# Tanh rows of additive attention: the column groups of one fill go to VectorE or GpSimd one by one

## The chip, the cores and the metric

The kernel runs on one core of a Trainium2 chip. The metric is the device time of one execution in microseconds (us). A core has four compute engines with instruction queues of their own: TensorE (PE in the profile, its weight loads PEld), VectorE (DVE), ScalarE (ACT) and GpSimd (POOL). Each works through its queue in order; between engines, semaphores hold an instruction until the data that it reads is there and the buffer that it writes is free. SyncE (SP) issues most DMAs.

## The reference

Everything is float32. There are 8 batches of 1024 tokens with 128 channels. Layer 0 is a convolution-like attention with 8 heads and two softmaxes, a layer norm, a feed-forward block and another layer norm. Layer 1 is what the change touches: additive attention, and then a recurrence.

```python
def _L1_attn_ref(B, W, v):
    Wi = jnp.einsum('bnd,ed->bne', B, W)
    scores = jnp.einsum('d,bijd->bij', v, jnp.tanh(Wi[:, None, :, :] + Wi[:, :, None, :]))
    attn = jax.nn.softmax(scores, axis=-1)
    return jnp.einsum('bij,bjd->bid', attn, B)

def step(yt, wx_t):                      # the recurrence, over 1024 tokens
    yt = jax.nn.sigmoid(wx_t + yt @ Vt)
    return (yt, yt)
```

For each pair (i, j) of tokens of a batch there are 128 sums, 128 tanh values and a weighted sum over the channels with `v`. The scores are symmetric in i and j, so the kernel computes one triangle.

## The kernel before

Channels lie on the 128 partitions, so `wiT` holds `Wi` of a batch as 128 x 1024. Token i gives one row: `tanh(wiT[:, i0:] + wiT[:, i])`. The 1024 tokens are cut into 8 row tiles `it` of 128 tokens. Row tile `it` needs w = 1024 − 128·it columns (a little less as one goes down in it, since the triangle starts at `begin[c]`). A **group** (function `group`, from line 978) is four **columns groups** c = 0 to 3 with k rows each, where k is 1 for row tiles 0 to 3, 2 for 4 and 5, 4 for 6, and 8 for 7. All of a group lies in one slot of the ring `th`, which has five slots of 128 x 4096 (three of them serve the first batch's narrow tiles).

A group can be made in two ways.

- ACT makes it directly (`tanh_row`, L1001): one tanh instruction for each row, with `wiT[:, i]` as its bias.
- DVE or POOL fills the slot with the sums, and then ACT does one wide tanh over the whole slot in place (L1047). POOL fills with one `tensor_tensor` for each of the four columns (`add_rows`, L1011). DVE fills with one `tensor_scalar` with an accumulator for each row where k is below 4 (`add_row`, L1005; the profile shows it as TENSOR_SCALAR_CACHE_REDUCE with a DVE_READ_ACCUMULATOR behind it), and with `add_rows`, four instructions, where k is 4 or 8.

Then PE multiplies the group's rows with `v` (`times_v`, L1064): the matmuls collect 128 tokens' scores in the PSUM tile `sa`, and the last one sets the slot free. When a pair of row tiles is complete, ACT takes the exponential out of `sa` (L1160), and the attention to B and the layer norm follow.

The order on every engine is not written by hand. The class `Plan` collects operations (`add`) with the engines that may do each, an estimated cost on each of them, a priority `pri`, what it reads and writes, and the slot that it takes or gives back. `emit` then plays the schedule through in Python when the program is built: it takes the engine that could start soonest, and among the operations that could start on it within 0.15 us of that the one with the lowest priority number, a handicap added that an engine's entry may carry. Only the resulting order goes to the chip; the chip's own durations decide when things really run. For an operation with several possible engines the choice is made in this play. `behind` holds an operation until others have begun. `port=True` marks DVE operations[...], and the play does not let the two run at once.

Layer 0 of batch b + 1 runs beside layer 1 of batch b; the priorities of both rise by one per batch, so that they advance together. The engines that may make a group are in the list `fillers`, which `layer1` writes for each group:

```python
if wide:
    fillers = [("ACT", 0.0)] + ([] if late else [("POOL", 0.0)]) + ([("DVE", 0.1)] if b < NB - 1 else [])
    if b == NB - 1:
        fillers += [("DVE", 0.1)]
elif it == NT // 2:
    fillers = [("DVE", 0.1), ("ACT", 0.1)] + ([] if late else [("POOL", 0.0)])
else:
    fillers = [("DVE", 0.1)] + ([("ACT", 0.1)] if early else [("POOL", 0.0)])
```

`wide` is row tile 0 to 3, `late` a row tile's last three groups, `early` the first and the last batch. In these two the narrow tiles (5, 6, 7) may thus be begun by DVE or ACT alone. In the other batches narrow row tiles share a pair with wide ones.

Before the change, the first operation of a group chooses among `fillers`, and all others of the group are bound to the engine that did the first (`placed`): 4k rows for ACT, 4k rows or 4 columns for DVE, 4 columns for POOL. Numbers that go beyond that vanish (`where` gives None).

Of the kernel before, what the change touches and what calls it, by code (L numbers as in the profile page):

```python
# [10 lines left out]
AF = mybir.ActivationFunctionType  # L11
# [402 lines left out]
class Plan:  # L414
# [24 lines left out]
    def add(self, where, fn, r=(), w=(), pri=0, mode="full", take=None, give=None, behind=(), wait=(), port=False):  # L439
        n = len(self.ops)  # L440
        deps = set()
        for k in r:
            if k in self.writer:
                deps.add(self.writer[k])
        for k in (*w, *wait):
            if k in self.writer:
                deps.add(self.writer[k])
            deps.update(self.readers.get(k, ()))
        for k in w:
            self.writer[k] = n  # L450
            self.readers[k] = []
        for k in r:
            if k not in w:
                self.readers.setdefault(k, []).append(n)
        deps.discard(n)
        self.ops.append((where, fn, (pri, n), mode, deps, take, give, behind, port))
        self.by.append(None)
        return n
# [107 lines left out]
def fast_path(ctx: ExitStack, tc: tile.TileContext, a: dict, fits):  # L566
# [5 lines left out]
    nc = tc.nc  # L572
# [16 lines left out]
    work = main.enter_context(tc.tile_pool(name="work", bufs=1))  # L589
# [126 lines left out]
    plan = Plan()  # L716
    add = plan.add
# [37 lines left out]
    count = {"aT": 0}  # L755
# [222 lines left out]
    def group(it, at0, r0, k, wiT, all_wi, L1, ROWS, fillers, chain, left, both, first_half):  # L978

        i0 = it * P
        w = N - i0
        g = count.setdefault("group", 0)
        count["group"] = g + 1
        slot = Bank(*slots[: 3 if first_half else 5])

        begin = [0 if r0 == 0 else 4 * r0 + c for c in range(4)]  # L990
        at = [k * sum(w - q for q in begin[:c]) for c in range(5)]

        def rows(c):
            return slot()[:, at[c] : at[c + 1]].rearrange("p (r n) -> p r n", r=k)

        def w_i(c, r=None):
            j = i0 + 4 * r0 + c
            return wiT[:, j : j + 4 * k - 3 : 4] if r is None else wiT[:, j + 4 * r : j + 4 * r + 1]

        def tanh_row(c, r):  # L1000
            nc.scalar.activation(rows(c)[:, r, :], wiT[:, i0 + begin[c] :], AF.Tanh, bias=w_i(c, r))  # L1001

        def add_row(c, r):

            nc.vector.tensor_scalar(  # L1005
                rows(c)[:, r, :], wiT[:, i0 + begin[c] :], w_i(c, r), 0.0, ALU.add, ALU.add, accum_out=unused
            )

        def add_rows(eng, c):
            shape = [P, k, w - begin[c]]  # L1010
            eng.tensor_tensor(  # L1011
                rows(c), wiT[:, i0 + begin[c] :].unsqueeze(1).to_broadcast(shape),
                w_i(c).unsqueeze(2).to_broadcast(shape), ALU.add,
            )


        each = [(c, r) for r in range(k) for c in range(4)]
        work = {
            "ACT": [(0.18 + 0.833e-3 * (w - begin[c]), lambda c=c, r=r: tanh_row(c, r)) for c, r in each],
            "POOL": [  # L1020
                (0.27 + 1.62e-3 * k * (w - begin[c]), lambda c=c: add_rows(nc.gpsimd, c)) for c in range(4)
            ],
            "DVE": [(0.21 + 1.05e-3 * (w - begin[c]), lambda c=c, r=r: add_row(c, r)) for c, r in each]
            if k < 4
            else [(0.15 + 1.04e-3 * k * (w - begin[c]), lambda c=c: add_rows(nc.vector, c)) for c in range(4)],
        }

        def does(i):
            return lambda e: work[e][i][1]()

        first = count[chain] = add(
            [(e, work[e][0][0], x) for e, x in fillers], does(0), r=all_wi, w=[("rows", g, 0)], pri=ROWS,
            take=slot, behind=[count[q] for q in (chain, *both) if q in count], port=k >= 4,
        )

        def placed(i):
            def where():
                e = plan.by[first]
                return (e, work[e][i][0]) if i < len(work[e]) else None

            return where

        for i in range(1, 4 * k):
            add(placed(i), does(i), w=[("rows", g, i)], pri=ROWS, behind=[first], port=k >= 4)
        add(
            lambda: None if plan.by[first] == "ACT" else ("ACT", 0.2 + 0.833e-3 * at[4]),
            lambda _: nc.scalar.activation(slot()[:, : at[4]], slot()[:, : at[4]], AF.Tanh),  # L1047
            r=[("rows", g, i) for i in range(4 * k)], w=[("tanh", g)], pri=ROWS - 0.02,
        )


        parts = []
        for s0 in range(0, N, 512):
            for c in range(4):
                s, s1 = max(s0, at0 + begin[c]), min(s0 + 512, at0 + w)
                if s < s1:
                    parts.append((c, s0, s, s1))
                    left[c, s0] = left.get((c, s0), 0) + k

        def times_v(_):  # L1060
            for r in range(k):
                for c, s0, s, s1 in parts:
                    left[c, s0] -= 1
                    nc.tensor.matmul(  # L1064
                        sa[32 * c : 32 * c + 32, s:s1], vpat[:, 31 - r0 - r : 63 - r0 - r],
                        rows(c)[:, r, s - at0 - begin[c] : s1 - at0 - begin[c]],
                        start=at0 + r0 + r == 0, stop=left[c, s0] == 0,
                    )

        n = -(-w // 512)
        before = ["sa"] if at0 and r0 == 0 else ["sa", "sa narrow"] if at0 else ["sa"] if r0 else []
        after = ["sa narrow"] if at0 and r0 == 0 else [] if r0 or at0 else ["sa"]
        add(
            ("PE", k * (1.69e-3 * (w - begin[0]) + 0.005 * n)), times_v, r=[("tanh", g)] + before,
            w=[("sa", it, r0)] + after, pri=L1, mode="groups", give=slot,
        )
        return ("sa", it, r0)
# [11 lines left out]
    E_first, at = {}, 0  # L1091
# [5 lines left out]
    def layer1(b):  # L1097
# [27 lines left out]
        for pair in order:  # L1125
# [19 lines left out]
            for s, it, at0, r0, k, fillers in sorted(todo):  # L1145
                ROWS = b + (past + n_blocks * s / 33) / len(E_first) / 4.5
                L1 = ROWS - 0.15
                keys.append(group(it, at0, r0, k, wiT, all_wi[:1] if early and pair[0] >= NT // 2 else all_wi, L1, ROWS, fillers, fills[it < NT // 2], left, fills if r0 == 0 else (), b == 0 and pair[0] >= NT // 2))
# [318 lines left out]
```

## Time and profile before

| What | us |
|---|---|
| median of 3 runs | 5683.9 (5677.94 to 5687.07) |
| profiled execution, its own time | 5681.58 |
| its span, first to last instruction | 5679.7 |
| layer 0 of the first batch alone | up to about 310 |
| layer 1 of one batch beside layer 0 of the next | about 392 to 4970 |
| last batch's layer 1, narrow row tiles | about 4970 to 5260 |
| last batch's layer 1, wide row tiles | about 5260 to 5590 |
| recurrence and output | from about 5590 |

The mean granted TensorE clock is 0.968 of full speed. DMA plays no part between the first load and the last stores: the queues took 1.5% or less of the DMA engines' time each.

A line of the groups part reads: source line, engine, operation, out<-in, shape, count | busy us in all, mean ns of one | idle us of the engine just before them, and what ended most of it. "POOL th L1011 <- PE sa L1064" in the waits means that a fill by POOL waited until PE's matmuls had freed its slot.

### The profile page before, as it was taken

How to read it: one execution, taken by the hardware profiler on the slowest of the kernel's cores; microseconds unless marked ns; L12 is line 12 of the kernel's file. 1: busy time of each engine (PE TensorE's matmuls, PEld its weight loads, DVE VectorE, ACT ScalarE, POOL GpSimd, SP SyncE). 2: the span in 40 equal slices, each digit the busy share in tenths (PEclk: the TensorE clock that was granted, in tenths of full speed). 3: DMA queues.
4: the chain of work that ended last, by engine and by line, in shares of the span. 5: the costliest groups of instructions: out<-in, count | busy, mean ns of one | idle time of the engine just before them, and what ended most of it. 6: DMA issues, size and time to landing. Idle time of an engine off the chain costs nothing.

```text
span 5679.7 us, 98799 instructions
## 1 busy us (share of the span) xinstructions
PE 5122.7 (90%) x39013; PEld 2778.3 (49%) x39013; DVE 5230.2 (92%) x8664; ACT 5172.3 (91%) x4498; POOL 4093.4 (72%) x2678
## 2 busy tenths in 40 slices
PE   8999999899999999899999999998998999975567
PEld 6655554545544455445544455554554455532125
DVE  7989999999999999999999999999998999998886
ACT  5489999799998999999999999998898999989994
POOL 2352787678868888778877888788686888862872
PEclk9999999999999999999999999999999999987998
DMA  2000000000000000000000000000000000000001
GB/s 60 1 5 1 1 1 5 1 8 1 1 5 5 5 1 5 1 9 1 1 5 5 5 1 5 1 8 1 1 1 5 5 1 1 11 19 7 1 1 64
DMA packets 27339, 37.88 MB, mean 7 GB/s; under 512 B 2465, under 2 KB 19233, under 8 KB 26865
## 3 DMA queue, kind: packets, MB, share of 16 engines
q1 hardware_dynamic: 24832, 27.99, 1.5%
q8 instruction: 308, 5.05, 0.4%
q10 hardware_dynamic: 1872, 3.16, 0.2%
q14 instruction: 167, 1.36, 0.1%
q0 software_dynamic: 160, 0.33, 0.0%
HBM read 19.41 MB, written 12.06 MB: 6 GB/s over the span
## 4 chain that ended last, share of the span: by engine, by line
PE 48%; DVE 30%; ACT 16%; issue 5%; POOL 1%; DMA 0%; DVEq 0%; ACTq 0%; SPq 0%; POOLq 0%
PE sa L1064 18%; PE m L906 10%; PE sc L857 8%; ACT th L1047 8%; DVE th L1005 7%; PE m L771 5%; ACT th L1001 5%; DVE stat_e L881 4%; DVE wx L868 3%; DVE stat_e L864 3%; DVE aT L783 3%; ACT wx L878 2%; PE m L835 1%; DVE stat_e L882 1%; ACT sc L860 1%
## 5 line engine op out<-in xcount | busy, mean ns | idle before, releaser
L1011 POOL TENSOR_TENSOR th<-wiT 128x1024 f32<-128x1024 f32 (+58 forms) x2088 | 3056.6, 1499 | 676.9 <-PE sa L1064 645.5
L1047 ACT ACTIVATE th<-th 128x3072 f32<-128x3072 f32 (+50 forms) x903 | 2496.1, 2795 | 86.4 <-DVE th L1005 79.0
L1064 PE MATMUL sa<-th,vpat 128*32 128x512 f32 (+34 forms) x24576 | 2079.0, 468 | 254.0 <-ACT th L1047 232.5
L1001 ACT ACTIVATE th<-wiT 128x398 f32<-128x398 f32 (+60 forms) x2444 | 1692.1, 764 | 84.3 <-PE sa L1064 83.2
L1005 DVE TENSOR_SCALAR_CACHE_REDUCE th<-wiT 128x288 f32<-128x288 f32 (+50 forms) x1760 | 1550.4, 881 | 159.4 <-PE sa L1064 44.5
L892 POOL TENSOR_TENSOR wx<-wx,stat_e 128x1024 f32<-128x1024 f32 x512 | 982.3, 1941 | 701.2 <-DVE stat_e L882 526.0
L1064 PEld LDWEIGHTS sa<-th,vpat 128*32 128x32 f32 x24576 | 665.9, 112 | 1427.9 <-issue 868.3
L857 PE MATMUL sc<-xT,wx 128*128 128x512 f32 x2048 | 990.5, 608 | 22.0 <-DVE wx L868 21.4
L906 PE MATMUL m<-aT,wx 128*128 128x256 f32 x3584 | 845.1, 389 | 10.1 <-DVE aT L783 8.7
L906 PEld LDWEIGHTS m<-aT,wx 128*128 128x128 f32 x3584 | 676.8, 193 | 196.5 <-issue 42.8
L868 DVE TENSOR_TENSOR wx<-sc,stat_e 128x1024 f32<-128x1024 f32 x512 | 623.5, 1218 | 23.9 <-DVE stat_e L865 0.5
L864 DVE TENSOR_REDUCE stat_e<-sc 128x16 f32<-128x1024 f32 x512 | 619.7, 1210 | 16.7 <-ACT sc L860 16.2
L783 DVE COPY aT<-m 128x512 f32<-128x512 f32 x932 | 603.1, 672 | 32.9 <-PE m L771 31.0
L771 PE MATMUL m<-ident,wx 128*128 128x128 f32 x3940 | 575.5, 280 | 56.7 <-DVE aT L783 30.2
L771 PEld LDWEIGHTS m<-ident,wx 128*128 128x128 f32 x3940 | 448.4, 142 | 362.9 <-issue 169.7
L860 ACT ACTIVATE sc<-sc 128x1024 f32<-128x1024 f32 x512 | 513.1, 1006 | 98.6 <-PE sc L857 88.2
L881 DVE TENSOR_REDUCE stat_e<-wx 128x128 f32<-128x2048 f32 x256 | 582.8, 2277 | 14.7 <-ACT wx L878 14.3
L878 ACT ACTIVATE wx<-wx 128x2048 f32<-128x2048 f32 x256 | 486.9, 1902 | 71.9 <-DVE wx L868 71.4
L857 PEld LDWEIGHTS sc<-xT,wx 128*128 128x128 f32 x2048 | 354.7, 191 | 403.3 <-issue 337.6
L882 DVE RECIPROCAL stat_e<-stat_e 128x128 f32<-128x128 f32 x256 | 243.9, 953 | 8.8
L739 POOL TENSOR_TENSOR stat<-stat,neg_half 128x4 f32<-128x4 f32 x64 | 65.2, 1019 | 134.8 <-DVE stat L736 115.1
L835 PEld LDWEIGHTS m<-Wvo,xT 128*128 128x128 f32 x1080 | 133.9, 193 | 58.0 <-issue 22.2
(172 smaller groups left out, 3065.7 us busy)
## 6 DMA issues: line engine op xcount, KB each, us to landing
xT<-in_xt_dram SPq DMA_DIRECT2D x8, 512.0 KB, 3.5
th<-in_x_dram SPq DMA_DIRECT2D x8, 512.0 KB, 7.0
parked<-X SPq DMA_DIRECT2D x16, 256.0 KB, 2.3
xr<-parked SPq DMA_DIRECT2D x8, 512.0 KB, 6.8
parked_wx<-bT SPq DMA_DIRECT2D x14, 256.0 KB, 2.0
wx<-parked_wx SPq DMA_DIRECT2D x7, 512.0 KB, 3.3
out_dram<-ot ACTq DMA_DIRECT2D x8, 256.0 KB, 2.2
out_dram<-ot SPq DMA_DIRECT2D x8, 256.0 KB, 2.5
```

Source lines behind the costliest of these rows:

```text
L771: nc.tensor.transpose(bank[:, i * P : (i + 1) * P], s, ident)
L857: nc.tensor.matmul(sc[:, cols], u[:, qt * P : (qt + 1) * P], xT[:, cols], start=True, stop=True)
L864: nc.vector.tensor_reduce(r1, sc.rearrange("p (m g) -> p g m", g=G), AX.X, ALU.add)
L868: nc.vector.tensor_tensor(e3, sc3, r1.unsqueeze(1).to_broadcast([P, M, G]), ALU.mult)
L881: nc.vector.tensor_reduce(r2, e2.rearrange("p q (m g) -> p q m g", g=G), AX.X, ALU.add)
L892: nc.gpsimd.tensor_tensor(e3, e3, r2[:, q, :].unsqueeze(2).to_broadcast([P, M, G]), ALU.mult)
L906: nc.tensor.matmul(bank()[:, :256], vp[:, t, :], aT[:, t, :], start=t == 0, stop=t == NT - 1)
L1001: nc.scalar.activation(rows(c)[:, r, :], wiT[:, i0 + begin[c] :], AF.Tanh, bias=w_i(c, r))
L1005: nc.vector.tensor_scalar(rows(c)[:, r, :], wiT[:, i0 + begin[c] :], w_i(c, r), 0.0, ALU.add, ALU.add, accum_out=unused)
L1011: eng.tensor_tensor(rows(c), wiT[:, i0 + begin[c] :].unsqueeze(1).to_broadcast(shape), w_i(c).unsqueeze(2).to_broadcast(shape), ALU.add,)
L1047: lambda _: nc.scalar.activation(slot()[:, : at[4]], slot()[:, : at[4]], AF.Tanh),
L1064: nc.tensor.matmul(sa[32 * c : 32 * c + 32, s:s1], vpat[:, 31 - r0 - r : 63 - r0 - r], rows(c)[:, r, s - at0 - begin[c] : s1 - at0 - begin ...
```

## The change

A group has four operations now instead of 4k, one for each column c, with all of its k rows. The first still chooses among `fillers`. If ACT takes it, ACT does the other three as well. If not, each of the columns 1 to 3 may go to POOL or to DVE, whatever `fillers` allows the first operation, and without a handicap for either; the play gives it to the one that could start sooner or has nothing more urgent. The wide tanh now reads from `filled` which stretches of the slot were filled. As a group is either ACT's or has all of its columns filled, that is the whole slot or nothing.

```diff
-        each = [(c, r) for r in range(k) for c in range(4)]
+        rows_of = range(k)
         work = {
-            "ACT": [(0.18 + 0.833e-3 * (w - begin[c]), lambda c=c, r=r: tanh_row(c, r)) for c, r in each],
...
+            "ACT": lambda c: (k * (0.18 + 0.833e-3 * (w - begin[c])), lambda: [tanh_row(c, r) for r in rows_of]),
+            "POOL": lambda c: (0.27 + 1.62e-3 * k * (w - begin[c]), lambda: add_rows(nc.gpsimd, c)),
+            "DVE": lambda c: (k * (0.21 + 1.05e-3 * (w - begin[c])), lambda: [add_row(c, r) for r in rows_of])
             if k < 4
-            else [(0.15 + 1.04e-3 * k * (w - begin[c]), lambda c=c: add_rows(nc.vector, c)) for c in range(4)],
+            else (0.15 + 1.04e-3 * k * (w - begin[c]), lambda: add_rows(nc.vector, c)),
         }
-        first = count[chain] = add(
-            [(e, work[e][0][0], x) for e, x in fillers], does(0), r=all_wi, w=[("rows", g, 0)], pri=ROWS,
-            take=slot, behind=[count[q] for q in (chain, *both) if q in count], port=k >= 4,
-        )
...
+        def filled():
+
+            runs = []
+            for c in range(4):
+                if plan.by[ops[c]] != "ACT":
+                    if runs and runs[-1][1] == c:
+                        runs[-1][1] = c + 1
+                    else:
+                        runs.append([c, c + 1])
+            return [(at[c], at[c1]) for c, c1 in runs]
+
+        def placed(c):
             def where():
-                e = plan.by[first]
-                return (e, work[e][i][0]) if i < len(work[e]) else None
+                if plan.by[ops[0]] == "ACT":
+                    return ("ACT", work["ACT"](c)[0])
+                return [(e, work[e](c)[0]) for e in ("POOL", "DVE")]
 
             return where
 
-        for i in range(1, 4 * k):
-            add(placed(i), does(i), w=[("rows", g, i)], pri=ROWS, behind=[first], port=k >= 4)
+        for c in range(4):
+            ops.append(add(
+                placed(c) if c else [(e, work[e](0)[0], x) for e, x in fillers], does(c), r=[] if c else all_wi,
+                w=[("rows", g, c)], pri=ROWS, take=None if c else slot, port=k >= 4,
+                behind=ops[:1] if c else [count[q] for q in (chain, *both) if q in count],
+            ))
+        count[chain] = ops[0]
+
+        def wide_tanh(_):
+            for a, z in filled():
+                nc.scalar.activation(slot()[:, a:z], slot()[:, a:z], AF.Tanh)
+
         add(
-            lambda: None if plan.by[first] == "ACT" else ("ACT", 0.2 + 0.833e-3 * at[4]),
-            lambda _: nc.scalar.activation(slot()[:, : at[4]], slot()[:, : at[4]], AF.Tanh),
-            r=[("rows", g, i) for i in range(4 * k)], w=[("tanh", g)], pri=ROWS - 0.02,
+            lambda: ("ACT", sum(0.2 + 0.833e-3 * (z - a) for a, z in filled())) if filled() else None,
+            wide_tanh, r=[("rows", g, c) for c in range(4)], w=[("tanh", g)], pri=ROWS - 0.02,
         )
```

More of the change, by code (lines that the diff above doesn't have):

```diff
@@ L1014, in add_rows @@
             )
-        each = [(c, r) for r in range(k) for c in range(4)]
+        rows_of = range(k)
         work = {
-            "ACT": [(0.18 + 0.833e-3 * (w - begin[c]), lambda c=c, r=r: tanh_row(c, r)) for c, r in each],
[L1020 to L1023, printed above, removed]
+            "ACT": lambda c: (k * (0.18 + 0.833e-3 * (w - begin[c])), lambda: [tanh_row(c, r) for r in rows_of]),
+            "POOL": lambda c: (0.27 + 1.62e-3 * k * (w - begin[c]), lambda: add_rows(nc.gpsimd, c)),
+            "DVE": lambda c: (k * (0.21 + 1.05e-3 * (w - begin[c])), lambda: [add_row(c, r) for r in rows_of])
@@ L1024, in group @@
             if k < 4
-            else [(0.15 + 1.04e-3 * k * (w - begin[c]), lambda c=c: add_rows(nc.vector, c)) for c in range(4)],
+            else (0.15 + 1.04e-3 * k * (w - begin[c]), lambda: add_rows(nc.vector, c)),
         }
-        def does(i):
-            return lambda e: work[e][i][1]()
-        first = count[chain] = add(
-            [(e, work[e][0][0], x) for e, x in fillers], does(0), r=all_wi, w=[("rows", g, 0)], pri=ROWS,
-            take=slot, behind=[count[q] for q in (chain, *both) if q in count], port=k >= 4,
-        )
@@ L1036, in placed, with does @@
-        def placed(i):
+        ops = []
+        def does(c):
+            return lambda e: work[e](c)[1]()
+        def filled():
[8 more added lines that the diff above has]
+        def placed(c):
             def where():
-                e = plan.by[first]
-                return (e, work[e][i][0]) if i < len(work[e]) else None
-            return where
```

## The prediction

> **What bounds the kernel now.** I read the page's first and fourth parts, then the busy time of each engine by stage, then the groups of instructions that write the ring `th`, then the waits and a few stretches of the timeline. All is set against the profiled execution's own time, 5681.6 us (its span is 5679.7).
>
> ```profile
> PE 5122.7 (90%) x39013; PEld 2778.3 (49%) x39013; DVE 5230.2 (92%) x8664; ACT 5172.3 (91%) x4498; POOL 4093.4 (72%) x2678
> PE 48%; DVE 30%; ACT 16%; issue 5%; POOL 1%; DMA 0%; DVEq 0%; ACTq 0%; SPq 0%; POOLq 0%
> ```
>
> Three engines are full and one is not, and the chain that ended last runs through the three full ones. GpSimd (POOL) is on 1% of it: its time is worth only what it takes off the others. The stages say where that can be (start and end, length, then busy us of PE, PEld, DVE, ACT and POOL with their instructions, clock, DMA):
>
> ```profile
> 392.00:600.00 208.00, 192.10 (x1436) 118.70 (x1432) 193.12 (x278) 196.15 (x387) 62.07 (x35) 0.99 0.00 1
> 600.00:4970.00 4370.00, 4121.13 (x31675) 2215.81 (x31671) 4103.49 (x6566) 4146.24 (x3236) 3494.49 (x2290) 0.98 0.01 4
> 4970.00:5260.00 290.00, 184.26 (x1747) 79.87 (x1742) 257.89 (x642) 257.50 (x283) 133.07 (x80) 0.80 0.04 12
> 5260.00:5590.00 330.00, 201.68 (x1985) 64.89 (x1981) 282.69 (x577) 308.01 (x122) 256.04 (x184) 0.93 0.00 1
> ```
>
> Before 392 no tanh rows are wanted (but for some at its end), after 5590 comes the recurrence: neither changes. In the long middle stage PE, ACT and DVE are each busy 94 to 95% and POOL 80%. In 4970 to 5260 (the last batch's narrow row tiles) PE has slack, DVE and ACT are 89% busy and POOL 46%. In 5260 to 5590 (its wide tiles) ACT is busy 93%, and all of that is the wide tanh.
>
> The work in question, by the page's groups (count, busy us, mean ns, idle before):
>
> ```profile
> L1011 POOL TENSOR_TENSOR th<-wiT 128x1024 f32<-128x1024 f32 (+58 forms) x2088 | 3056.6, 1499 | 676.9 <-PE sa L1064 645.5
> L1047 ACT ACTIVATE th<-th 128x3072 f32<-128x3072 f32 (+50 forms) x903 | 2496.1, 2795 | 86.4 <-DVE th L1005 79.0
> L1001 ACT ACTIVATE th<-wiT 128x398 f32<-128x398 f32 (+60 forms) x2444 | 1692.1, 764 | 84.3 <-PE sa L1064 83.2
> L1005 DVE TENSOR_SCALAR_CACHE_REDUCE th<-wiT 128x288 f32<-128x288 f32 (+50 forms) x1760 | 1550.4, 881 | 159.4 <-PE sa L1064 44.5
> ```
>
> POOL fills 2088 columns, 522 groups; 903 groups have a wide tanh, so DVE fills 381; 2444 rows go to ACT directly. The 645.5 us that POOL waits for PE are waits for a free slot: fills are not short of POOL but of buffers. ACT waits for DVE's fills (79.0), hardly for POOL's. The plainest place is the last batch's narrow tiles:
>
> ```profile
> 5102.11 1.02 POOL L739 TENSOR_TENSOR stat<-stat,neg_half 128x4 f32<-128x4 f32 x1 [8.02 <-DVE stat L736]
> 5212.59 14.72 POOL L1011 TENSOR_TENSOR th<-wiT 128x1020 f32<-128x1020 f32 x8 [109.46 <-PE sa L1064]
> ...
> 5155.17 2.33 ACT L1047 ACTIVATE th<-th 128x2548 f32<-128x2548 f32 x1 [1.65 <-DVE th L1005]
> 5157.40 2.00 ACT L1001 ACTIVATE th<-wiT 128x62 f32<-128x62 f32 x8
> 5160.29 2.27 ACT L1047 ACTIVATE th<-th 128x2484 f32<-128x2484 f32 x1 [0.89 <-DVE th L1005]
> ```
>
> POOL stands for 109.46 us, because there it may not begin a group, while DVE fills alone and ACT alternates between a tanh that has to wait for DVE and direct rows at 0.25 us for 62 elements.
>
> [...]DVE rows take 1.18 to 1.20 us at 933 to 952 elements while POOL is filling. [...]L1166 shows the price, 1237 ns on average for 128 elements where the similar L1170, with one input in PSUM, takes 268. [...]here it is 1.7 us (6.80 for four columns from 930) against about 1.3 with the accumulator read and the gap, 1.3 times. [...]here five direct rows of 911 take 4.81 us, four so 3.85, and one wide tanh over 3674 elements 3.25.
>
> **The change part by part.**
>
> 1. Groups that DVE begins may get help from POOL. In 4970 to 5260 ACT does 216 direct rows in 88.5 us and waits 23.5 us for DVE's rows. DVE needs about 0.65 us a row in row tile 5 (8 rows, 5.2 us a group); with two columns on POOL some 2.7, and DVE has the difference for a group that ACT does directly now. In row tile 7 the 8 direct rows at 0.25 us, four times over, make 8 us a group, a wide tanh at most 3.6 (4096 elements): 4.4 us saved for each of three groups, 13 us. Row tiles 6 and 4, estimated from the same timeline: two groups and six groups with some 2 and 1.3 us each, 12 us. Of the waits I take back half, 12 us. Sum 37; 35 us is taken. Bounds: 0 (DVE still begins few more groups) and 60 (all overhead and waits gone, then the tile's PE work at a clock of 0.80 is late next).
> 2. The first batch's narrow tiles (392 to 600): POOL is idle 146 us and ACT does 328 direct rows, but DVE is 93% busy with layer 0 and begins few groups (16 rows and 8 columns there). 5 us, bounds 0 and 20.
> 3. The wide tiles at the end: ACT waits 13.0 us for DVE in the stage; the rest is its own work, which stays. 0, bounds −5 and 10.
> 4. The middle stage. Two flows meet. DVE-begun groups are slow: the rows 936, 935, 934, 933 of one group start at 2556.82, 2558.14, 2569.79 and 2571.01, a slot held 15 us for 5 us of work. POOL can take the later columns. Against it, in groups that POOL begins the DVE's handicap of 0.1 is gone for columns 1 to 3, so it takes columns that POOL would have done. POOL's 1818 columns there are 455 groups, with 1365 such columns; DVE's 1218 rows and 24 columns are some 260 groups, with about 780. I take the net transfer as zero: POOL, 80% busy, is free within a column's time and takes most of the second kind, DVE a third of the first. What stays is that groups finish sooner and slots turn faster. If a fifth of POOL's 876 idle us is used, at 1.46 us a column (2652 us over 1818) that is 120 columns, 30 groups that ACT need not do directly, 0.6 us each (3.85 less 3.25): 18 us of ACT, of which I count 15. Bounds: PE is idle 249 us in the stage, so a gain over 110 is not to be had; a loss up to 90, from the rival below.
> 5. Edits with one answer: the wide tanh stays one instruction over the whole group (a group not begun by ACT has all four columns filled); ACT's direct rows become one piece per column, which alters nothing at one row a column, as in row tiles 0 to 3. Where it waits for two engines, the slower counts. No DMA is moved. A DVE column in a group that POOL began waits for PE to free the slot; layer 0's reductions and evictions stand behind it on DVE, PE's transposes behind those. Now such waits are 44.5 us. I take no more, at worst 45 again, inside the loss above.
>
> Sum: 35 + 5 + 0 + 15 = 55 us, 5681.6 − 55 = 5626.6. The median before is 2.3 us above the profiled execution, so 5629.
>
> **Rivals.**
>
> - *DVE is relieved.* POOL takes 250 columns more from DVE than it gives. A row costs DVE 0.91 us (1109 us over 1218 rows), so 227 us less on an engine with 30% of the chain: 68, and with 18 of ACT and 40 from the two narrow stretches 126: 5558. For: DVE's gaps are so small that it is the fullest engine, and POOL stands 438 us for slots between 600 and 4900. Against: a waiting POOL has no slot to fill unless DVE opened one.
> - *DVE takes POOL's work*, the slower case. Each column that moves to DVE costs it 0.91 us or more, since the handicap that sent it to POOL is gone, and POOL merely waits longer for slots. From a net 147 columns (40 / (0.91 × 0.30)) it eats the gain of the narrow stretches; at 350 it is 96 − 40 = 56 us lost: 5740. For: a column is open in most moments, and every one that DVE takes puts 1.2 us ahead of layer 0. Against: layer 0's priority stops it once layer 0 falls behind.
> - *Nothing comes of it*: the two flows and their waits cancel, as far as a fully loaded PE lets anything be seen: 5684.
>
> **How the numbers follow.** The likeliest, some 30 to 75 us gained (5609 to 5654), 0.40; DVE relieved 0.19; slower 0.30; no difference 0.11. This kernel's measurement can tell about 0.2%, 11 us. So faster 0.59, same 0.11, slower 0.30; time 5629. The range takes most of both large rivals: 5540 to 5740; the likeliest's own is 5609 to 5654.
>
> **What would show it.** Right, if POOL's pause of 109 us near 5100 is filled, direct rows of L1001 fall under 2300, ACT's 79 us of waits for DVE's fills shrink, and the wide tanh's count rises over 930. DVE's fill rows should stay between 1550 and 1950 in number: far above, the slower rival is at work, far below, the faster. If POOL's busy time falls under 3900 and DVE's idle waits on PE double, the prediction is wrong in its fourth step.

## The result

The changed kernel takes 5547.3 us (median of 4 runs, 5541.3 to 5550.6); the kernel before took 5680.9 us beside it. The ratio is 0.9762, with a 95% interval of 0.9746 to 0.9779: 133.6 us gained, where 55 were forecast. The profiled execution has a span of 5547.8 us.

The first lines are those of the page's parts 1 and 4, for the changed kernel:

```profile
PE 5065.5 (91%) x39013; PEld 2769.0 (50%) x39013; DVE 5151.6 (93%) x8414; ACT 5120.7 (92%) x4263; POOL 4373.5 (79%) x2876
PE 50%; DVE 32%; ACT 12%; issue 4%; POOL 1%; DMA 0%; DVEq 0%; ACTq 0%; POOLq 0%; SPq 0%
```

POOL is busy 280 us more, DVE 79 and ACT 52 less. The groups that make the rows, for the changed kernel (the wide tanh has moved to L1059, the matmuls to L1079):

```profile
L1011 POOL TENSOR_TENSOR th<-wiT 128x1024 f32<-128x1024 f32 (+59 forms) x2286 | 3338.2, 1496 | 428.7 <-PE sa L1079 412.8
L1059 ACT ACTIVATE th<-th 128x2292 f32<-128x2292 f32 (+57 forms) x933 | 2567.8, 2781 | 75.6 <-DVE th L1005 57.9
...
L1001 ACT ACTIVATE th<-wiT 128x504 f32<-128x504 f32 (+61 forms) x2180 | 1574.0, 795 | 25.1 <-PE sa L1079 25.0
L1005 DVE TENSOR_SCALAR_CACHE_REDUCE th<-wiT 128x952 f32<-128x952 f32 (+59 forms) x1627 | 1448.4, 890 | 143.7 <-PE sa L1079 32.5
```

POOL does 198 columns more, DVE 133 rows less, and ACT 264 direct rows less, in exchange for 30 more wide tanhs. On ACT that is 118 us less of direct rows and 72 us more of wide tanh, and 70 us less waiting before the two.

The exponentials of `sa` end a row tile or pair and so serve as milestones. From the timeline of the kernel before: the first batch's last narrow tile, the last exponential of the seventh batch, the last batch's last narrow tile, and its last wide one.

```profile
625.61 0.37 ACT L1160 ACTIVATE E<-sa 128x256 f32<-128x256 f32 x1
5057.90 0.58 ACT L1160 ACTIVATE E<-sa 128x512 f32<-128x512 f32 x1
5230.74 0.37 ACT L1160 ACTIVATE E<-sa 128x256 f32<-128x256 f32 x1
5583.23 0.70 ACT L1160 ACTIVATE E<-sa 128x640 f32<-128x640 f32 x1 [2.07 <-PE sa L1064]
```

The same four in the changed kernel:

```profile
572.23 0.41 ACT L1175 ACTIVATE E<-sa 128x256 f32<-128x256 f32 x1
4959.69 0.58 ACT L1175 ACTIVATE E<-sa 128x512 f32<-128x512 f32 x1
5107.69 0.36 ACT L1175 ACTIVATE E<-sa 128x256 f32<-128x256 f32 x1
5453.67 0.70 ACT L1175 ACTIVATE E<-sa 128x640 f32<-128x640 f32 x1 [1.20 <-PE sa L1079]
```

From these: **first** (start to the first milestone) 53 us gained, **middle** (first to second) 45, **last narrow** (second to third) 25, **last wide** (third to fourth) 6, the rest 2. The subtraction says where time is missing in this pair of executions. Whether the sharing of columns took it away is a question for experiments.

The milestones follow layer 1 alone, and layer 0 of the next batch, which runs beside it, does not share in the first stage's lead. ACT's exponentials of layer 0 (L860, 64 a batch) up to the first milestone, in the kernel before and in the changed one:

```profile
0.00:625.60 625.60, 96.24 (x96) 0.99 0.06 15
```

```profile
0.00:572.20 572.20, 86.44 (x86) 1.00 0.06 17
```

The 96th begins at 624.7 us before and at 641.1 after the change. So layer 1 is 53 us ahead there and layer 0 is 16 us behind; the 53 us are not all won.

### The profile page after: what moved, and what is told of

Read it like the earlier page. It is cut to its first block, busy times and chain, and to the rows that moved or that the text cites. A ratio compares the mean times of both kernels' runs of the same rounds, so it can differ in the third digit from the quotient of the medians.

```text
span 5547.8 us, 98978 instructions
## 1 busy us (share of the span) xinstructions
PE 5065.5 (91%) x39013; PEld 2769.0 (50%) x39013; DVE 5151.6 (93%) x8414; ACT 5120.7 (92%) x4263; POOL 4373.5 (79%) x2876
## 4 chain that ended last, share of the span: by engine, by line
PE 50%; DVE 32%; ACT 12%; issue 4%; POOL 1%; DMA 0%; DVEq 0%; ACTq 0%; POOLq 0%; SPq 0%
PE sa L1079 18%; PE m L906 10%; PE sc L857 9%; DVE th L1005 7%; ACT th L1059 7%; PE m L771 5%; DVE stat_e L881 4%; DVE wx L868 3%; DVE stat_e L864 3%; ACT th L1001 3%; DVE aT L783 3%; PE m L835 2%; DVE X L743 1%; DVE stat_e L882 1%; PE m L821 1%
## 5 line engine op out<-in xcount | busy, mean ns | idle before, releaser
L1011 POOL TENSOR_TENSOR th<-wiT 128x1024 f32<-128x1024 f32 (+59 forms) x2286 | 3338.2, 1496 | 428.7 <-PE sa L1079 412.8
L1059 ACT ACTIVATE th<-th 128x2292 f32<-128x2292 f32 (+57 forms) x933 | 2567.8, 2781 | 75.6 <-DVE th L1005 57.9
L1079 PE MATMUL sa<-th,vpat 128*32 128x512 f32 (+31 forms) x24576 | 2051.4, 465 | 224.0 <-ACT th L1059 206.1
L1001 ACT ACTIVATE th<-wiT 128x504 f32<-128x504 f32 (+61 forms) x2180 | 1574.0, 795 | 25.1 <-PE sa L1079 25.0
L1005 DVE TENSOR_SCALAR_CACHE_REDUCE th<-wiT 128x952 f32<-128x952 f32 (+59 forms) x1627 | 1448.4, 890 | 143.7 <-PE sa L1079 32.5
L1079 PEld LDWEIGHTS sa<-th,vpat 128*32 128x32 f32 x24576 | 662.9, 111 | 1364.6 <-issue 871.0
L860 ACT ACTIVATE sc<-sc 128x1024 f32<-128x1024 f32 x512 | 513.5, 1008 | 81.2 <-PE sc L857 72.8
```

Of the source, the lines that this page charges most:

```text
L1005: nc.vector.tensor_scalar(rows(c)[:, r, :], wiT[:, i0 + begin[c] :], w_i(c, r), 0.0, ALU.add, ALU.add, accum_out=unused)
L1011: eng.tensor_tensor(rows(c), wiT[:, i0 + begin[c] :].unsqueeze(1).to_broadcast(shape), w_i(c).unsqueeze(2).to_broadcast(shape), ALU.add,)
L1059: nc.scalar.activation(slot()[:, a:z], slot()[:, a:z], AF.Tanh)
L1079: nc.tensor.matmul(sa[32 * c : 32 * c + 32, s:s1], vpat[:, 31 - r0 - r : 63 - r0 - r], rows(c)[:, r, s - at0 - begin[c] : s1 - at0 - begin ...
```

## Experiments

Every run's time stands beside runs of the kernel before on the same chip, with a median of 5681 to 5687 us. The stages of all runs are in the table after the last experiment.

### Which batches, and what the new form does without sharing

A group has operations by column in all four; only where columns may be shared differs. Bound columns come, in effect, to this, with e0 for the engine of column 0:

```diff
-                return [(e, work[e](c)[0]) for e in ("POOL", "DVE")]
+                return (e0, work[e0](c)[0])
```

In the other three the columns are shared in some batches (the first of the two lines) and bound in the rest.

> The new form of a group (one operation per column with all of its k rows), but columns 1 to 3 are bound to the engine that did column 0, in every batch. Nothing is shared. Theory A (the gain is the sharing): no change, 5681 within 11 us. Theory C (the gain comes from coarser pieces and another order, the play of the schedule simply falling out better): at least 40 of the 133 us are there already, 5640 or less.

> Columns are shared in the first batch alone. In the changed kernel layer 1 of the first batch is 53 us ahead when its narrow tiles are done (exponential of row tile 6 at 572.2 instead of 625.6), while layer 0 of the third batch starts 21 us earlier (912 instead of 933). Theory A (what a stretch gains is kept to the end): 53 us gained, 5628. Theory B (layer 0 sets the pace, the lead of layer 1 is eaten up): 21 us or less, 5660 or more.

> Columns are shared in the last batch alone. Between the exponentials at 5057.9 and 5583.2 before the changed kernel gains 31 us (25 of them in the narrow tiles). Theory A: 31 us gained, 5650. Theory B: the same 31, as nothing follows but the recurrence. My prediction's first step had 35. Under 20 or over 45 would say that the last batch's start hangs on how the batch before it ended.

> Columns are shared in batches 1 to 6 alone, with layer 0 beside them throughout. Theory A: the 45 us that the changed kernel gains between the exponentials at 625.6 and 5057.9, 5636. Theory B (the middle is where all engines are full, and the first batch's lead is not kept): 70 to 100 us gained, 5580 to 5610. The prediction's fourth step had 15: 5666.

Measured: bound 5586.3 (ratio 0.9823, 0.9806 to 0.9839), first batch alone 5647.5 (0.9938, 0.9919 to 0.9958), last batch alone 5562.3 (0.9777, 0.9761 to 0.9793), middle alone 5643.2 (0.9924, 0.9908 to 0.9941). Theory A falls at once, and theory C has the bound run on its side: with nothing shared 100 us are gained. But no theory foresaw the rest: sharing in the first batch or the middle, beside bound columns elsewhere, gives times **worse** than bound columns everywhere. (The middle's 5643 lies near the 5636 of theory A, but it is 57 us more than bound columns take.) The stages show why the sum fails. First batch alone does finish its narrow tiles early (576.2 against 634.6 with bound columns), and all of its first batch (last exponential at 1094.4 against 1170.6). But from there to the second milestone, where the rule is the same as in the bound kernel, it takes 3930 us, and the bound kernel 3804. The same rule, started from another point, differs by 126 us. Last batch alone and bound run alike, within 5 us, up to the last batch, and there sharing gains 17 us (5568.2 against 5585.6 in span).

So the middle stage has a spread of its own, as large as the effect in question, and two causes were left: coarser pieces are worth something, or the order happened to fall out well.

### How far near-ties move the time

```diff
-    LATENCY = {"PE": 0.6, "ACT": 0.5, "DVE": 0.4, "POOL": 0.6, "SP": 8.0}
+    LATENCY = {"PE": 0.6, "ACT": 0.5, "DVE": 0.401, "POOL": 0.6, "SP": 8.0}
```

In the second of the four, ACT's 0.5 became 0.501 instead.

> The kernel before, with DVE's latency in the play of the schedule at 0.401 us instead of 0.400. No rule changes; only near-ties in the play fall otherwise, and the order of instructions with them. The run with bound columns gained 100 us though its rule gives DVE and POOL nothing new. Theory D (the schedule's play is so sensitive that any small change moves the time by tens of us): between 5590 and 5720, off 5684 by over 15 us. Theory C (coarser pieces really gain): within 11 us of 5684.

> The kernel before, with ACT's latency in the play at 0.501 us instead of 0.500. As the run before: theory D expects a time off 5684 by over 15 us and off the other such run, theory C one within 11 us of 5684.

> Bound columns (nothing shared), with DVE's latency in the play at 0.401 us. Theory C (coarser pieces are worth 100 us): near 5586. Theory D (the 100 us were a lucky order[...]): most of it gone, 5620 to 5690.

> The changed kernel, with DVE's latency in the play at 0.401 us. If sharing is what gains, it stays clear of all orders without sharing but the lucky one: 5520 to 5590. If the 133 us were mostly luck: 5600 or more.

Measured: the kernel before 5663.8 (0.9965, 0.9949 to 0.9981) and 5649.1 (0.9937, 0.9914 to 0.9959), bound 5617.7 (0.988, 0.9851 to 0.9908), changed 5559.9 (0.9778, 0.975 to 0.9807). A thousandth of a microsecond in the play of the schedule moves the finished kernel by 13 to 35 us. Theory D holds for the two copies of the kernel before. Bound lost 31 of its 100 us: 2 us short of D's range, and far from the "most of it gone" that D had said. The changed kernel stays clear of all orders without sharing, the bound ones too, but not of "last batch alone" with its 5562. The spread alone does not make bound columns as slow as the kernel before, so a cause that differs between orders was looked for.

DVE is busy 66 us less with bound columns than in the kernel before, and 53 of these lie in five groups of short instructions. Four of the five are marked `port`: in the play none of them overlaps an operation of POOL. Two in the kernel before, from its groups:

```profile
L1166 DVE TENSOR_TENSOR E<-E,half 128x128 f32<-128x128 f32 x64 | 77.6, 1237 | 6.6 <-ACT E L1160 6.6
L743 DVE TENSOR_SCALAR B<-X,stat 128x128 f32<-128x128 f32 x64 | 55.7, 931 | 0.0
```

The same two with bound columns:

```profile
L1183 DVE TENSOR_TENSOR E<-E,half 128x128 f32<-128x128 f32 x64 | 53.0, 852 | 5.5 <-ACT E L1177 5.5
L743 DVE TENSOR_SCALAR B<-X,stat 128x128 f32<-128x128 f32 x64 | 32.7, 573 | 0.0
```

Shapes and counts are the same, the mean is a third less. The longest case, in the timeline of the kernel before:

```profile
3953.11 14.26 DVE L1166 TENSOR_TENSOR E<-E,half 128x128 f32<-128x128 f32 x1
3954.81 12.41 POOL L1011 TENSOR_TENSOR th<-wiT 128x853 f32<-128x853 f32 x8
3967.29 1.21 DVE L868 TENSOR_TENSOR wx<-sc,stat_e 128x1024 f32<-128x1024 f32 x1
```

A product of 128 elements takes 14.26 us: POOL's eight fills follow one another without a gap, and it ends only when they do. Layer 0 stands behind it on DVE. Added up over the five groups (this product, the three normalisations of L743 and the addition of eps, L736) DVE spends 312 us in the kernel before, 296 and 297 in its copies, 259 and 269 with bound columns, 259 in "last batch alone" and 300 in "first batch alone". The middle's length goes with it: 4432, 4416 and 4412; 4340, 4362 and 4344; 4448. Where columns are shared in the middle it does not go along: 305, 305 and 314, at a middle of 4388, 4393 and 4391. What the five groups last beyond their own time is called their port waits, after the keyword; that a port is the cause is not shown. That the waits make the length is argued so far; the next runs take the five groups off DVE.

### Which direction of sharing pays, and the five groups off DVE

The first two of these four share columns only in groups that DVE began, or only in those that POOL began. The other two move the five groups to POOL, in the kernel before and in the changed one. The lines below are an excerpt; the entries of the play (engine, cost, `port`) change with them, and the scale and shift behind a normalisation become an operation of their own, which stays on DVE:

```diff
-            nc.vector.tensor_scalar(rs, mv[:, :, 1], EPS, None, ALU.add)
+            nc.gpsimd.tensor_scalar(rs, mv[:, :, 1], EPS, None, ALU.add)
...
-                nc.vector.tensor_scalar(dst[:, j, :], src[:, j, :], mv[:, j, 0:1], rs[:, j : j + 1], ALU.subtract, ALU.mult)
+                nc.gpsimd.tensor_scalar(dst[:, j, :], src[:, j, :], mv[:, j, 0:1], rs[:, j : j + 1], ALU.subtract, ALU.mult)
...
-                add(("DVE", 0.28), lambda _, D=D: nc.vector.tensor_tensor(D, D, half, ALU.mult),
+                add(("POOL", 0.6), lambda _, D=D: nc.gpsimd.tensor_tensor(D, D, half, ALU.mult),
```

> The changed kernel, but a group that POOL began is filled by POOL alone; groups that DVE began are shared. Theory R (the gain is that POOL relieves DVE's groups): the narrow stage of the first batch done near 572, the middle near 4390 us, 5540 to 5590. Theory P (the gain is that both directions shorten the fill): about half of it, 5600 to 5640.

> The changed kernel, but a group that DVE began is filled by DVE alone; groups that POOL began are shared, with no handicap for DVE. Theory R: no gain over the kernel before and its near copies, 5640 to 5700, the narrow stage of the first batch done near 630, and possibly slower, as the slower rival of the prediction had it (DVE takes POOL's work). Theory P: about half of the gain, 5600 to 5640.

> The kernel before, with three small operations moved from DVE to POOL: the layer norms' (x - mean) * rstd, the addition of eps, and the product of E's diagonal block with half. [...] Theory L (these waits are what differs between orders): DVE's busy time falls by 250 us or more and 100 to 180 us are gained, 5500 to 5585. Theory D (order as such, no single cause): under 60 us gained, over 5620.

> The changed kernel with the same three operations on POOL. Theory L: faster than the changed kernel by 60 to 130 us, 5420 to 5490, and 60 to 110 us faster than the kernel before with the same edit, which is then what sharing is worth. If POOL, busy 79% already, becomes the bound: 5550 or more.

Measured: DVE-begun alone 5576.4 (0.9809, 0.9784 to 0.9835), POOL-begun alone 5678.3 (0.9988, 0.9981 to 0.9995). Theory R holds for the two totals, but its first stages missed: 597 where 572 was expected, and 658 where 630 was. DVE's and POOL's fills where DVE-begun groups are shared:

```profile
L1011 POOL TENSOR_TENSOR th<-wiT 128x1024 f32<-128x1024 f32 (+56 forms) x2346 | 3426.6, 1495 | 375.6 <-PE sa L1080 337.6
L1005 DVE TENSOR_SCALAR_CACHE_REDUCE th<-wiT 128x652 f32<-128x652 f32 (+58 forms) x1543 | 1385.5, 898 | 179.5 <-PE sa L1080 72.0
```

And where POOL-begun groups are:

```profile
L1011 POOL TENSOR_TENSOR th<-wiT 128x1024 f32<-128x1024 f32 (+53 forms) x2037 | 2967.8, 1489 | 766.8 <-PE sa L1080 750.9
L1005 DVE TENSOR_SCALAR_CACHE_REDUCE th<-wiT 128x512 f32<-128x512 f32 (+58 forms) x1830 | 1631.4, 891 | 135.0 <-PE sa L1080 16.5
```

In the first, POOL takes 258 columns more than before (2088) and DVE has 217 rows less (1760). In the second DVE takes work that POOL had time for: 70 rows more, 51 columns less, and POOL merely waits for slots 105 us longer (750.9 against 645.5). The slower rival's mechanism exists, then, and the stages show its cost: 658 us up to the first milestone, where all other runs have 572 to 640, and 396 us for the last wide tiles, where all others have 338 to 359. In these last tiles DVE fills 336 rows instead of 294 and POOL 161 columns instead of 196, and the wide tanh waits for DVE. The kernel before, 5231 to 5583 us:

```profile
ACT th L1047 <- DVE th L1005: 13.2, 12, 1.8
```

POOL-begun groups shared, 5181 to 5577 us:

```profile
ACT th L1060 <- DVE th L1005: 46.1, 39, 2.0
```

A middle and last narrow tiles as short as those of the other sharing runs (4387 and 136) make up for it in the total. These two runs do not bear out that the middle goes with the five groups either: 327 us of them at 4393, 274 at 4387.

The five groups on POOL: kernel before 5522.6 (0.9715, 0.9699 to 0.9731), changed kernel 5457.3 (0.96, 0.9584 to 0.9616). Theory L holds for the times: 162 us come from three small edits to operations that have nothing to do with the tanh rows. DVE's busy time falls 180 us, from 5230.2. The 250 us that were expected are not reached, since DVE has used part of the time for 88 fill rows more (60 us) and spends 58 us more in the scale and shift of the layer norms (see the last experiment):

```profile
PE 5074.2 (92%) x39013; PEld 2758.7 (50%) x39013; DVE 5049.8 (91%) x8459; ACT 5161.4 (93%) x4484; POOL 4263.3 (77%) x2994
```

The edits take two things off DVE at once, the operations' own time and their waits. An estimate from the fast ones among them in the kernel before (the tenth percentile of each group, 0.17 to 0.33 us, times its count) puts their own time at some 114 us, so about 200 are waits.

### The pair again, and scale and shift on POOL

The first three repeat the comparison without the five groups on DVE: bound columns, and the two kernels with the 0.401. The fourth moves the scale and shift of both layer norms of layer 0 to POOL too, in the changed kernel with the five groups on POOL (the first norm's lines; the second's are changed alike):

```diff
-                    nc.vector.tensor_tensor(Xg, Xg, over_tiles(g1_sb, 4), ALU.mult)
-                    nc.vector.tensor_tensor(Xg, Xg, over_tiles(be1_sb, 4), ALU.add)
+                    nc.gpsimd.tensor_tensor(Xg, Xg, over_tiles(g1_sb, 4), ALU.mult)
+                    nc.gpsimd.tensor_tensor(Xg, Xg, over_tiles(be1_sb, 4), ALU.add)
...
```

> Bound columns (nothing shared) with the three operations on POOL, as in x1_before. Theory L[...]: the advantage is gone with the waits, within 25 us of x1_before, 5500 to 5550. Theory C (coarser pieces are worth something by themselves): 5460 or less, at least 60 us under x1_before.

> x1_before with DVE's latency in the play at 0.401 us. If the orders differ mostly by the port waits, this stays within 20 us of 5522; if order as such moves the time, it may be anywhere from 5490 to 5555.

> x2_after with DVE's latency in the play at 0.401 us. Sharing really worth some 65 us: 5440 to 5475, with the first batch's narrow tiles done near 580 and a middle of about 4285 us. If the pair was lucky: 5480 or more.

> x2_after with the layer norms' scale and shift over 512 elements on POOL as well (32 products, 32 sums). In x1_before one such product takes 2.4 us on DVE where 1 us was usual[...]. Theory L: some 60 us less on DVE, 10 to 40 us gained, 5415 to 5447. POOL, then 84% busy, as the next bound: 5460 or more.

Measured: bound 5540.1 (0.9743, 0.9726 to 0.9759), kernel before 5529.8 (0.9727, 0.9711 to 0.9743), changed 5430.4 (0.9551, 0.9535 to 0.9567), scale and shift moved 5398.5 (0.9496, 0.948 to 0.9512). The changed kernel came out below the 5440 to 5475 that were expected of its copy, and the last run below its 5415 to 5447. The advantage of bound columns is gone: they are the slowest of the three that share nothing, so with the five groups away coarser pieces gain nothing that shows. The edit is worth 162 and 134 us in the kernel before and its copy and 46 with bound columns. The operations moved are the same in all three, in shape and count, so their own time (estimated above at 114 us) does not explain that difference; fewer port waits fit it. But bound columns save only 53 us in the five groups, and how these became 100 us is not shown in full. Sharing stands: 5430 and 5457 against 5523, 5530 and 5540, on average 5444 against 5531, 87 us. Near-ties still move the changed kernel by 27 us.

One thing that may make a wait dearer than its length is in the traces. PE runs out of work during the 14.26 us of the case above (it stands idle for 11.76 us, until 3971.63), and its granted clock is 0.51 of full speed for the 14 us after 3963 (PE, PEld, DVE, ACT and POOL, then the clock):

```profile
3963.00:3977.00 14.00, 5.15 (x13) 2.80 (x14) 13.62 (x16) 2.06 (x2) 4.22 (x3) 0.51 0.00 0
```

The shortest spells at half clock in the two traces of the pair last 3.4 us. In the middle stage every spell at half clock begins behind 3.4 us in which PE was busy 51% at most in the kernel before (29% on average) and 46% at most in the changed kernel (22%). Such spells add up to 205 us in the first and 133 in the second. In the other direction, of the 53 stretches of 3.4 us in the middle of the kernel before in which PE was busy less than half, 49 are followed by half clock. The granted clock over the whole execution is 0.968 in the kernel before, 0.975 with bound columns, 0.979 in the kernel before with the five groups on POOL and 0.980 in the changed kernel. How much of the kernel's time this costs, beside the waits themselves, no run separates.

The last run is the fastest version of all, 288 us under the kernel before. One line of the kernel before with the five groups on POOL:

```profile
L932 DVE TENSOR_TENSOR X<-X,ln_g_sb 128x512 f32<-128x512 f32 x16 | 43.4, 2711 | 0.0
```

And the line in its place in the last run:

```profile
L932 POOL TENSOR_TENSOR X<-X,ln_g_sb 128x512 f32<-128x512 f32 x16 | 20.5, 1281 | 1.3
```

On DVE the product took 2711 ns on average (1050 in the kernel before with all on DVE), on POOL itself 1281. The move is worth 59 us against 5457, more than the 40 expected at most, and 32 against the near copy's 5430.

Stages of all runs in us, by the four milestones (profiled executions; "five groups" is their sum on DVE):

| Kernel | time | first | middle | last narrow | last wide | five groups |
|---|---|---|---|---|---|---|
| before | 5680.9 | 626 | 4432 | 173 | 352 | 312 |
| before, DVE 0.401 | 5663.8 | 625 | 4416 | 170 | 352 | 296 |
| before, ACT 0.501 | 5649.1 | 627 | 4412 | 162 | 353 | 297 |
| bound | 5586.3 | 635 | 4340 | 162 | 353 | 259 |
| bound, 0.401 | 5617.7 | 630 | 4362 | 168 | 356 | 269 |
| first batch shared | 5647.5 | 576 | 4448 | 163 | 356 | 300 |
| last batch shared | 5562.3 | 632 | 4344 | 153 | 342 | 259 |
| middle shared | 5643.2 | 630 | 4393 | 164 | 356 | 305 |
| DVE-begun shared | 5576.4 | 597 | 4393 | 143 | 347 | 327 |
| POOL-begun shared | 5678.3 | 658 | 4387 | 136 | 396 | 274 |
| changed | 5547.3 | 572 | 4388 | 148 | 346 | 305 |
| changed, 0.401 | 5559.9 | 572 | 4391 | 166 | 338 | 314 |
| before, five groups on POOL | 5522.6 | 628 | 4280 | 154 | 359 | on POOL |
| same, 0.401 | 5529.8 | 627 | 4303 | 144 | 359 | on POOL |
| bound, five groups on POOL | 5540.1 | 640 | 4286 | 156 | 357 | on POOL |
| changed, five groups on POOL | 5457.3 | 583 | 4289 | 135 | 347 | on POOL |
| same, 0.401 | 5430.4 | 581 | 4262 | 139 | 346 | on POOL |
| and scale and shift | 5398.5 | 583 | 4233 | 135 | 347 | on POOL |

## Why the prediction was off

The direction was right and the time fell inside the range, near its lower end, but the gain was 2.4 times the forecast one. The likeliest case's own range, 5609 to 5654, missed. By its steps:

**Step 2, the first batch's narrow tiles, is the one that failed.** It took 5 us, with 20 as its bound, because DVE "begins few groups"; 53 came at the milestone, and 44 to 63 wherever kernels with full sharing there stand beside kernels without any, the five groups being on DVE or on POOL in both. The argument took the number of groups that DVE begins as given. It is not: from 392 us to the milestone DVE begins four narrow groups before the change and ten after it, as POOL does about half of each. And it left out what such a group did to its slot in the meantime. Before, one group's rows on DVE (timeline; widths 344 to 341, one for each column, and then the four again):

```profile
466.80 0.56 DVE L1005 TENSOR_SCALAR_CACHE_REDUCE th<-wiT 128x344 f32<-128x344 f32 x1
...
471.99 0.48 DVE L1005 TENSOR_SCALAR_CACHE_REDUCE th<-wiT 128x343 f32<-128x343 f32 x1
...
483.02 0.56 DVE L1005 TENSOR_SCALAR_CACHE_REDUCE th<-wiT 128x342 f32<-128x342 f32 x1
...
486.07 0.57 DVE L1005 TENSOR_SCALAR_CACHE_REDUCE th<-wiT 128x341 f32<-128x341 f32 x1
```

Twenty microseconds for eight rows of 0.56, in one of three slots. In the changed kernel the group with begin 352 has two columns on POOL beside two on DVE:

```profile
441.22 2.66 POOL L1011 TENSOR_TENSOR th<-wiT 128x702 f32<-128x702 f32 x2 [6.27 <-PE sa L1079]
```

```profile
443.95 0.57 DVE L1005 TENSOR_SCALAR_CACHE_REDUCE th<-wiT 128x352 f32<-128x352 f32 x1
...
446.15 0.58 DVE L1005 TENSOR_SCALAR_CACHE_REDUCE th<-wiT 128x350 f32<-128x350 f32 x1
```

It is complete in 5.5 us. Six narrow groups more are filled from 392 us to the milestone (eleven wide tanhs of them instead of five), and ACT does not make them row by row. ACT's direct rows up to the first milestone, in the kernel before and in the changed one:

```profile
392.00:626.00 234.00, 142.45 (x366) 0.99 0.00 1
```

```profile
392.00:572.00 180.00, 102.28 (x268) 0.99 0.01 1
```

Forty microseconds less of them, against some 14 more of wide tanh, on an engine that was busy 196 of 208 us there. The mechanism that step 4 named for the middle, a slot held long for little work, applied here most, and it was not carried over. Not all of the 53 us is won, since layer 0 has fallen 16 us back by then. How much of the lead is lost again in the middle is not shown, so steps 2 and 4 are safest read together: 20 us forecast, 98 measured in this pair, 64 on average with the five groups on POOL.

**Step 1, the last batch's narrow tiles:** 35 forecast, 25 measured; 11 between the averages of the kernels and their near copies (168 and 157), 14 with the five groups on POOL (151 and 137). The pause of 109 us on POOL is filled, as the prediction asked; the longest left is 28 us:

```profile
5098.28 11.87 POOL L1011 TENSOR_TENSOR th<-wiT 128x1024 f32<-128x1024 f32 x5 [28.34 <-PE sa L1079]
```

**Step 3, the last wide tiles:** 0 forecast, 6 measured, and 11 with the five groups on POOL. Small, and of the right kind: ACT waited 13 us for DVE's fills there before and 2 us after.

**Step 4, the middle:** 15 forecast, 45 measured between the two executions, and the runs do not show that sharing earned them. With the five groups on POOL the middle lasts 4280, 4303 and 4286 without sharing and 4289 and 4262 with it: 14 us apart on average, less than orders differ. With them on DVE, it depends on the order: 4340 to 4432 in the kernels that share nothing, 4388 and 4391 in the changed one and its copy. The chosen size fits the 14. "The net transfer as zero" does not fit quite: between the two milestones POOL fills 136 columns more (120 were forecast), DVE 80 rows less, and ACT makes 61 rows less, half of the 30 groups that step 4 counted. The lower bound rested on DVE against POOL for columns, and it missed that other instructions of DVE last longer beside POOL's: in the kernel before 177 of the 384 in the five groups outlast one POOL instruction and take 227 us. The prediction had read that price in one product (L1166, 1237 ns for 128 elements, where L1170 takes 268) and did not count it here.

**The rivals.** "DVE is relieved", at 5558, came closest in time and in part in mechanism: DVE fills 133 rows less, where it asked for 250, and sharing only the groups that DVE began is 108 us under the kernel before, though only 10 under bound columns. DVE is busy 79 us less, not 227, and ACT's direct rows fall by 264. The slower case's transfer is real when it stands alone (70 more rows on DVE), and cost time in the first stage and the last wide tiles.

**What would show it:** direct rows 2180, under 2300; wide tanhs 933, over 930; DVE's rows 1627, within 1550 to 1950; ACT's waits for DVE's fill rows 57.9 after 79.0. All held, so these signs told the direction and not the size.

In sum, sharing is worth some 87 us in the runs with the five groups on POOL (by stages about 50 up to the first milestone, 14 in the middle, 14 and 11 in the last two; the stages come from the profiled executions and add up to 2 more). With them on DVE, the changed kernel and its copy are on average 111 us under the kernel before and its two copies, and 48 under the two with bound columns. So the miss has two parts. The 87 us alone are 1.6 times the forecast, mostly by step 2. The rest of the 133.6 came with the order in which this pair happened to meet, which is luck: the kernel before is the slowest of three near copies, the changed one the faster of two. How the 133.6 divide is the best reading of the runs, not shown for this pair.

## What to carry to other kernels

- Let a second engine finish what the first has begun, rather than only begin work of its own. Here the fills got shorter, DVE could begin more of them, and most was moved where the helper had been idle and only three buffers served.
- Where a program's order comes from a greedy play of a schedule, change a constant by a thousandth and measure before explaining a few per cent; compare families of orders, not two kernels. And where two streams share the engines, look at both before a milestone of one is called a gain.
- Look at the mean of small instructions across runs. The five groups took 312 us here, by the estimate 114 of them their own; 186 of their 384 instructions outlasted one or more of POOL's, and moving them to POOL was worth more in the kernel before than the change under study (162 us against 133.6).

## What was not expected of the hardware

One product of 128 elements on DVE (L1166) stayed behind a whole row of POOL instructions: it took 14.26 us, where the tenth percentile of its group is 0.28, and ended with the eighth fill. Most cases are shorter. Of the 384 instructions of the five groups in the kernel before, 198 end without a POOL instruction ending in their time. 177 outlast one and end before the next does, in 118 of these cases although POOL's next one follows at once. Five outlast two, and four outlast four to nine. Why some end after POOL's first instruction and others only after several is not shown. Most of the time is lost behind a single POOL instruction: the 177 take 227 us, the four longest 34. The play's `port` rule, by which the two never overlap there, doesn't prevent either, as only its order reaches the chip.
